# Reordering the work around three seams of a two-layer graph network: first batches, last attention batch with layer 1's first aggregate, and the last stages

## The chip, the cores and the metric

The kernel runs on one core of a Trainium2 chip. The metric is the device time of one execution in microseconds (us), lower is better. All arithmetic is float32. The engines are named as in the profile: PE is TensorE (matmul and transpose), PEld its weight loads, DVE is VectorE, ACT is ScalarE, POOL is GpSimd, and SP is the engine that issues most of the transfers (DMA). [...]

## The reference

The input x holds 16 batches of 1024 nodes with 256 channels; adj is one 1024 x 1024 matrix. Cut to what matters:

```
# layer 0
c_adj = mean of x over channels
A     = 2*| |sigmoid(c_adj[i]-c_adj[j]) - 0.5| - 0.5 |          # symmetrised
g     = relu((x^T @ (adj * A)) * para)                           # queries
k, v  = x @ kv_w
x     = layernorm(x + softmax(q @ k^T * scale) @ v)              # 4 heads of 64
# layer 1
A_norm = adj + I
dinv   = rsqrt(column sums + row sums - diagonal of A_norm)
A_hat  = A_norm * dinv[:, None] * dinv[None, :]
agg    = A_hat @ x
h      = relu(batchnorm(agg @ W1.T + b1))                        # 512 features
out    = batchnorm(h @ W2.T + b2)
return layernorm(x + out)
```

Both batchnorms take their statistics over all 16 x 1024 rows, so each of them is a point that all batches must have passed.

## The kernel before, in words

The tensors lie with 128 rows on partitions; a batch's x is a tile of 128 x 8 x 256 (1 MB). Score tiles are 128 x 1024 and take two PSUM banks; the others take one bank of 128 x 512. PSUM has three pools of two buffers each in the attention: s (scores and pg), t (transposes, keys, values, denominators) and o (attention outputs).

PE, ACT and DVE follow a written order (`manual_schedule`): their instructions run in the order in which the code emits them. SP and POOL follow theirs too, through the queues. So the order around the change is set by the loops of `run(list, k)`, which emit the next k steps of a list.

- **Start (L1144 to L1157).** `prologue(b)` (L757) makes three lists for a batch: `first` (`begin`, which sums x over channels on DVE at L772, writes the means to DRAM and reads them back as a row on all partitions at L779 and L781; and the four transposes of x, L788), `steps` (values L877, keys L864, then the graph matmuls L827) and `side` (the graph weights: ACT at L808 and L813, DVE at L817). Batch 0's and batch 1's lists are mixed here by hand; for batch 1 all of `side` is emitted before `steps`.
- **Attention.** A batch has two pairs of heads, two halves of queries and eight chunks of keys: 32 units, taken two at a time, so 16 bursts a batch (u = 0 to 15). A burst emits the scores of its two units (L924, exp on ACT at L929) and then the outputs of the burst before (L945, with the sums of the denominators on DVE, acc, L952 and L954). When all chunks of one half of the queries are done, outputs become oT (ACT copies one bank at L958, DVE adds the other at L959). `normalise` (L967) sums the denominators on PE, copies them on ACT and sends them through DRAM into columns (dcol). `residual` takes the reciprocal (L988), transposes oT (poT, L991), multiplies on DVE (o, L995) and adds to x on POOL (L1000). `statistics_x1` is the layernorm's bn_stats on DVE (16 small instructions, L614) and four POOL steps (L587 to L618, rs and nm); `finish_x1` applies it with 8 ACT instructions (L622) and stores the batch from POOL's queue (x1_d).
- **Last batch (b = 15).** The bursts carry, instead of a next batch, the preparation of layer 1, from the dict `last` (L1173): the transposes of the adjacency (`transpose_adjacency`, pah, L1071; ACT moves them to ahT at L1074 and sums the columns), the degrees (DVE L1081 to L1084, POOL's power at L589, and a row of dinv through DRAM), the transposes of W1 and W2 (pw, L1039 and L1048, copied to w12T by DVE), the identity's addition on POOL (L1093) and the scaling of ahT by dinv (`scale_adjacency`, DVE L1096, eight of them). The weights are loaded at u = 6 of b = 14.
- **First aggregate (L1252 to L1262).** `aggregate_first(m)` (pagg, L1123) sums batch 0 over the eight m, with scaling m+1 emitted before step m; the last denominators and residuals of b = 15 come at m = 1 and 4; `adjacency_sums` (aT, L691 to L694) and the layernorm of b = 15 come behind. ACT copies pagg to agg_0 (L1129).
- **Layer 1 loop (b = 1 to 15).** Strassen-like products of seven: `aggregate(b)` (a_agg, b_agg, c_agg, L1341) with the steps of `linear1(b - 1)` (a_h, b_h, c_h, L1373) mixed in, two a step; `linear1` begins with sums tT on DVE. h goes to DRAM by POOL's queue.
- **Second product.** The linear step of batch 15 (ph, L1452) is plain; `coefficients1` makes the batchnorm's scale and shift. Then, for each batch, h is loaded by SP (`load_h`, pool hl), scaled with relu on ACT (L1442), multiplied (po2 tiles, written po in the profile, L1512), moved by DVE with the bias (L1523), and summed for statistics (L1527).
- **Final stage.** For each batch: scale and shift on ACT (L1554), transposes back (pf, L1577) with x_1 added on DVE, or, for the other half, on PE (held, L1563 and L1592); layernorm coefficients in ten small POOL steps (L1604 to L1613); then two pieces of the result on DVE (L1620) and six on ACT (L1625), and one store of 1 MB from SP's queue (L1629).

## Time and profile before

| | |
|---|---|
| median of 3 runs | 2630.38 us (2630.32 to 2632.36) |
| profiled execution | 2630.78 us |
| its span | 2628.9 us |
| granted PE clock, mean | 0.996 |

The span splits into stages by the lines that run: the start up to about 76 us; batches to 1622; the last batch's bursts to 1703.6; the first aggregate to 1736.6; the layer 1 loop to 2286 (36.4 a batch); ph to 2301; the second product to 2526; the final stage to 2629.

How to read it. Times are microseconds from the span's start. In a row such as "L954 DVE TENSOR_TENSOR acc<-acc,p ... x384 | 484.7, 1262" the line number belongs to the listing above, the tile names are the program's, x384 is the count, 484.7 the busy time in total and 1262 the mean of one in nanoseconds. In a list of waits, "PE pah L1071 <- DVE o L995" says which instruction stood and whose end released it, followed by the total, the number of times and the longest. A busy PE is not PE at its peak, since matmuls overlap. Of the three engines that follow the written order, the page shows these groups with idle time before them:

```profile
L929 ACT ACTIVATE p<-ps 128x1024 f32<-128x1024 f32 x512 | 496.8, 1023 | 192.8 <-PE ps L924 161.7
L954 DVE TENSOR_TENSOR acc<-acc,p 128x1024 f32<-128x1024 f32 x384 | 484.7, 1262 | 126.9 <-ACT p L929 98.0
L924 PE MATMUL ps<-qT,kT 64*64 64x512 f32 x4096 | 490.6, 592 | 0.6 <-DVE qT L836 0.3
L945 PE MATMUL po<-p,v 64*64 64x512 f32 x4096 | 488.0, 589 | 0.0
```

### The profile page before, as it was taken

The page shows a single profiled execution, that of the slowest core. Times are in us where ns is not written, and L with a number is a line of the kernel's source. Part 1 is how long each engine was busy: PE and PEld are TensorE (multiplying, and loading weights), DVE is VectorE, ACT ScalarE, POOL GpSimd, SP SyncE. Part 2 cuts the span into 40 slices and gives each one's busy share as a digit, 9 for nine tenths or more (in the row PEclk, how much of TensorE's full clock was granted, in tenths as well). Part 3 has the DMA queues.
Part 4 walks back from the last instruction along what each step waited for, and adds up shares of the span by engine and source line. Part 5 has one row for each costly group of instructions (what it writes and reads, how often), then busy time and mean ns, then how long its engine had stood idle before and what let it go on. Part 6 is the DMA issues. An engine that isn't in the chain of part 4 may idle for free.

```text
span 2628.9 us, 32328 instructions
## 1 busy us (share of the span) xinstructions
PE 2565.4 (98%) x13158; PEld 1130.2 (43%) x13158; DVE 1515.3 (58%) x1941; ACT 1202.5 (46%) x1479; POOL 362.0 (14%) x439
## 2 busy tenths in 40 slices
PE   8999999999999999999999999999999999999986
PEld 4443443444434434444344444344444444444455
DVE  4365665655756646556566466766565565533367
ACT  6365564664655646646656564511010110133358
POOL 0010110101101101011011010331221122000035
PEclk9999999999999999999999999999999999999999
DMA  4001101011011011010110110111221222253458
GB/s 144 1 9 41 33 10 41 17 25 33 10 41 33 9 41 31 12 41 2 41 33 9 41 49 2 41 65 80 96 96 64 96 80 96 96 216 142 153 197 300
DMA packets 134559, 168.98 MB, mean 64 GB/s; under 512 B 86784, under 2 KB 120064, under 8 KB 124032
## 3 DMA queue, kind: packets, MB, share of 16 engines
q1 hardware_dynamic: 129568, 116.47, 14.0%
q0 software_dynamic: 4832, 50.34, 4.6%
q8 instruction: 105, 1.72, 0.3%
q14 instruction: 54, 0.44, 0.1%
HBM read 99.36 MB, written 67.44 MB: 63 GB/s over the span
## 4 chain that ended last, share of the span: by engine, by line
PE 83%; DVE 8%; ACT 6%; issue 1%; DMA 1%; POOL 0%; DVEq 0%; POOLq 0%; ACTq 0%
PE ps L924 16%; PE pg L827 16%; PE po L945 16%; PE po L1512 8%; PE pv L877 5%; PE b_agg L1341 4%; PE c_agg L1341 4%; PE pk L864 3%; PE b_h L1373 2%; PE a_agg L1341 2%; PE c_h L1373 2%; ACT o L1625 1%; ACT o L1554 1%; PE pxT L788 1%; PE den L967 1%
## 5 line engine op out<-in xcount | busy, mean ns | idle before, releaser
L929 ACT ACTIVATE p<-ps 128x1024 f32<-128x1024 f32 x512 | 496.8, 1023 | 192.8 <-PE ps L924 161.7
L954 DVE TENSOR_TENSOR acc<-acc,p 128x1024 f32<-128x1024 f32 x384 | 484.7, 1262 | 126.9 <-ACT p L929 98.0
L924 PE MATMUL ps<-qT,kT 64*64 64x512 f32 x4096 | 490.6, 592 | 0.6 <-DVE qT L836 0.3
L945 PE MATMUL po<-p,v 64*64 64x512 f32 x4096 | 488.0, 589 | 0.0
L827 PE MATMUL pg<-wg,x 128*128 128x512 f32 x960 | 420.9, 594 | 0.0
L1000 POOL TENSOR_TENSOR x<-x,o 128x512 f32<-128x512 f32 x64 | 123.1, 1924 | 1173.5 <-DVE o L995 1173.5
L945 PEld LDWEIGHTS po<-p,v 64*64 64x64 f32 x4096 | 159.9, 133 | 280.2 <-issue 271.5
L827 PEld LDWEIGHTS pg<-wg,x 128*128 128x128 f32 x960 | 178.9, 190 | 221.5 <-issue 208.5
L924 PEld LDWEIGHTS ps<-qT,kT 64*64 64x64 f32 x4096 | 152.6, 133 | 282.7 <-issue 254.4
L1512 PE MATMUL po<-hl,w12T 128*128 128x512 f32 x512 | 222.0, 596 | 3.4 <-DVE bn_st L1527 2.7
L836 DVE SCALAR_TENSOR_TENSOR qT<-pg,para_s 128x1024 f32<-128x1024 f32 (+1 forms) x34 | 39.2, 1160 | 236.2 <-PE pg L827 235.0
L817 DVE SCALAR_TENSOR_TENSOR wg<-wg,adj_s 128x1024 f32<-128x1024 f32 x128 | 162.1, 1278 | 22.9 <-ACT wg L813 22.9
L1512 PEld LDWEIGHTS po<-hl,w12T 128*128 128x128 f32 x512 | 97.7, 191 | 127.7 <-issue 120.9
L808 ACT ACTIVATE wg<-crow,ccol 128x1024 f32<-128x1024 f32 x128 | 147.1, 1150 | 9.3 <-DMA crow<-c 9.3
L813 ACT ACTIVATE wg<-wg 128x1024 f32<-128x1024 f32 x128 | 136.2, 1065 | 1.7
L1442 ACT ACTIVATE hl<-hl,bn_sh,bn_sg 128x1024 f32<-128x1024 f32 x64 | 74.3, 1229 | 137.1 <-DMA hl<-h 125.2
L877 PE MATMUL pv<-kvw_s,xT 128*128 128x256 f32 x512 | 126.9, 391 | 8.3 <-ACT kT L868 8.3
L959 DVE TENSOR_TENSOR oT<-po,oT 128x512 f32<-128x512 f32 x64 | 44.2, 691 | 145.6 <-ACT oT L958 145.6
L864 PE MATMUL pk<-xT,kvw_s 128*128 128x512 f32 x256 | 121.7, 598 | 3.3 <-ACT v L882 3.3
L1523 DVE TENSOR_SCALAR o<-po,col_b 128x1024 f32<-128x1024 f32 x31 | 39.8, 1284 | 137.9 <-PE po L1512 137.9
L622 ACT ACTIVATE x<-x,nm_l,rs_l 128x256 f32<-128x256 f32 x128 | 64.6, 587 | 111.4 <-POOL nm_l L618 111.4
L877 PEld LDWEIGHTS pv<-kvw_s,xT 128*128 128x128 f32 x512 | 92.6, 189 | 52.2 <-ACT kT L868 27.5
(163 smaller groups left out, 2698.0 us busy)
## 6 DMA issues: line engine op xcount, KB each, us to landing
h<-hw POOLq DMA_DIRECT2D x16, 2048.0 KB, 6.6
hl<-h SPq DMA_DIRECT2D x15, 2048.0 KB
x<-x POOLq DMA_DIRECT2D x16, 1024.0 KB, 4.2
x1l<-x SPq DMA_DIRECT2D x16, 1024.0 KB
xf<-x SPq DMA_DIRECT2D x16, 1024.0 KB
out_dram<-o SPq DMA_DIRECT2D x16, 1024.0 KB
x<-in_x_dram SPq DMA_DIRECT2D x15, 1024.0 KB
crow<-c SPq DMA_DIRECT2D x15, 512.0 KB
```

The costliest lines, as they stand in the source:

```text
L808: nc.scalar.activation(w, s["crow"], AF.Abs, bias=s["ccol"][:, n : n + 1])
L813: nc.scalar.activation(w, w, AF.Tanh, scale=0.5)
L817: nc.vector.scalar_tensor_tensor(w, w, 1.0, adj_s[:, n, :], op0=ALU.subtract, op1=ALU.mult)
L827: nc.tensor.matmul(s["pg"][:, hs], xt[:, n, c * P : (c + 1) * P], s["wg", n][:, hs], start=(n == 0), stop=(n == NCH - 1),)
L864: nc.tensor.matmul(ps, kvw_s[:, c, kc * P : (kc + 1) * P], s["xT"][:, c, hs], start=(c == 0), stop=(c == CC - 1),)
L877: nc.tensor.matmul(pt[:, j * C : (j + 1) * C], s["xT"][:, c, n * P : (n + 1) * P], kvw_s[:, c, C : 2 * C], start=(c == 0), stop=(c == CC - 1),
L924: nc.tensor.matmul(ps[kh * D : (kh + 1) * D, hd * HALF : (hd + 1) * HALF], kT[r, pr, ks], qT[r, pr, qh * HALF : (qh + 1) * HALF], start=Tr ...
L929: nc.scalar.activation(p, ps, AF.Exp)
L945: nc.tensor.matmul(g["po"][kh][hd * D : (hd + 1) * D, :], s["v"][r, m, h * D : (h + 1) * D], p[r, hd * HALF : (hd + 1) * HALF], start=(m = ...
L954: nc.vector.tensor_add(g["acc"], g["acc"], p)
L1341: nc.tensor.matmul(ps, left, right, start=(start and i == 0), stop=(i == NCH // 2 - 1), skip_group_check=True,)
L1512: nc.tensor.matmul(ps[:, hs], w2T[:, k, c * P : (c + 1) * P], h[k][:, hs], start=(k == 0), stop=(k == HC - 1),)
```

## The change

It moves instructions and splits a few of them; the sums that the kernel computes stay.

- Start: batch 1's `begin` is emitted after the fifth of batch 0's first eight steps; batch 1's steps and side work are emitted one and one.
- Last batch: one adjacency group (two halves) in each of the bursts 0 to 7; the weights' load at burst 1 of b = 15; residuals at bursts 2, 9 and 13; batch 14's statistics at burst 11 and its apply and store at burst 12; x1l loads at bursts 6 and 13; the scaling of m = 0 and 1 at burst 14, of m = 2 among the last outputs, of m = 3 to 7 at the first aggregate's first step. The aggregate's sums lie in single banks of the pools o and t, the last denominators and poT in pool s.
- Batch 15's statistics come right after the first aggregate; its apply, its store and the load of x1l_2 come in the first step of the loop's b = 1, and the linear steps of batch 0 start one step later (three of them in two of the steps).
- One `manual_schedule` spans all stages after the attention. ph is summed by halves; the pool hl is opened ahead of o2p; the first po2 batch takes k = 0, 1 of both channel groups, then k = 2, 3; the last channel group of the last batch is summed by halves.
- Final stage: the x_1 tiles 3 to 6 and 10 to 13 are loaded as pairs into hl's buffers. For batch 15, batch 14's `finish` comes ahead of its coefficients, which are made on DVE except for the power; DVE makes four pieces and ACT four; the store is split into two halves, from SP's and ACT's queue.

The diff, with what only moves by indentation or renames left out:

```diff
@@ outputs(i), L946
+            if i < len(units) - 1:
+                sums()
...
+            if i == len(units) - 1:
+                scale_adjacency(2)
+                sums()
@@ normalise, residual
+            den = tile_s("den_last")[:, H0] if last else tile_t(f"den_{k}")
...
+            if (b, pr) == (B - 1, PAIRS - 1):
+                pt = tile_s(f"poT_{k}")[:, H0]
@@ -1117,16 +1128,17 @@
                 agg[0] = xTp.tile([P, CC, N], F32, tag="xT", name="agg_0")
-                agg["ps"] = [tile_s(f"pagg_{c}") for c in range(CC)]
-            for c in range(CC):
-                for hs in (H0, H1):
+                agg["ps"] = [[tile(f"pagg_{i}") for i in range(2)] for tile in (tile_o, tile_t)]
+            for c in (1, 0):
+                for half, hs in enumerate((H0, H1)):
                     nc.tensor.matmul(
-                        agg["ps"][c][:, hs], x1l[0][:, m, c * P : (c + 1) * P], aht[m][:, hs],
+                        agg["ps"][c][half], x1l[0][:, m, c * P : (c + 1) * P], aht[m][:, hs],
...
             if m == NCH - 1:
-                for c in range(CC):
-                    nc.scalar.copy(agg[0][:, c, :], agg["ps"][c])
+                for c in (1, 0):
+                    for half, hs in enumerate((H0, H1)):
+                        nc.scalar.copy(agg[0][:, c, hs], agg["ps"][c][half])
@@ -1144,17 +1156,20 @@
             next_first, next_steps, next_side = prologue(1)
-            for _ in range(8):
+            for i in range(8):
...
                 run(side, 2)
-            run(next_first, 5)
+                if i == 4:
+                    run(next_first, 1)
+            run(next_first, 4)
...
                     run(next_side, 3)
-            run(next_side, 99)
-            run(next_steps, 8)
+            for _ in range(8):
+                run(next_steps, 1)
+                run(next_side, 1)
@@ -1170,20 +1185,14 @@
-            last = {
-                0: [(transpose_adjacency, (m, h)) for m in (0, 1) for h in (0, 1)],
-                4: [(transpose_adjacency, (m, h)) for m in (2, 3) for h in (0, 1)],
-                6: [(transpose_adjacency, (m, h)) for m in (4, 5) for h in (0, 1)],
-                8: [(transpose_adjacency, (m, h)) for m in (6, 7) for h in (0, 1)],
-                5: [(load_x1l, (0,))],
-                7: [(load_x1l, (1,))],
-                9: [(degrees, ())],
-                10: [(transpose_weights, ())],
-                12: [(add_identity, ())],
-                15: [(scale_adjacency, (0,))],
-            }
+            last = {u: [(transpose_adjacency, (u, h)) for h in (0, 1)] for u in range(NCH)}
+            for u, todo in (
+                (1, (load_weights,)), (6, (load_x1l, 0)), (9, (degrees,)), (10, (transpose_weights,)),
+                (12, (add_identity,)), (13, (load_x1l, 1)), (14, (scale_adjacency, 0)),
+                (14, (scale_adjacency, 1)),
+            ):
+                last.setdefault(u, []).append((todo[0], todo[1:]))
             before_last = {
-                6: [(load_weights, ())],
@@ -1206,14 +1215,14 @@
                         run(sums, 1)
-                    elif u in (2, 4, 12):
+                    elif u in (2, 9, 13):
                         run(full, 2)
-                    elif u == 5:
-                        run(late, 1)
-                    elif u == 7:
-                        run(late, 1)
...
                         run(sums, 1)
+                    elif u == 11:
+                        run(late, 1)
+                    elif u == 12:
+                        run(late, 1)
@@ -1250,16 +1259,22 @@
             for m in range(NCH):
-                if m + 1 < NCH:
-                    scale_adjacency(m + 1)
+                if m == 0:
+                    for k in range(3, NCH):
+                        scale_adjacency(k)
+                elif m < 4:
+                    adjacency_sums(m - 1)
+                elif m == 4:
+                    adjacency_sums(3)
...
                     run(full, 2)
-            for i in range(NCH // 2):
-                adjacency_sums(i)
-            run(late, 2)
+            late.clear()
+            x_last = st.pop(B - 1)["x"]
+            last_statistics, last_apply = layernorm_steps(x_last, f"l0_{B - 1}")
+            last_statistics()
@@ -1285,15 +1300,19 @@
+    manual = ExitStack()
+    manual.enter_context(tc.manual_schedule(engines={PE, Activation, DVE}))
@@ -1413,10 +1432,10 @@
         for b in range(1, B):
-            if b + 1 < B:
+            if 1 < b < B - 1:
...
                 x1_sums(b + 1)
-            else:
+            elif b == B - 1:
@@ -1427,7 +1446,13 @@
                     later = linear1(b)
-                run_linear(lin, 2)
+                if b > 1 or i > 0:
+                    run_linear(lin, 3 if b == 1 and i in (3, 5) else 2)
+                if b == 1 and i == 0:
+                    last_apply()
+                    nc.gpsimd.dma_start(x1_d[B - 1], x_last)
+                    load_x1l(2)
+                    x1_sums(2)
@@ -1447,21 +1472,21 @@
             ps = [bank(f"ph_{k}_{half}") for half in range(2)]
-            for c in range(CC):
-                for half, hs in enumerate((H0, H1)):
+            for half, hs in enumerate((H0, H1)):
+                for c in range(CC):
...
                     )
-            if k == HC - 1:
-                scale_shift1(h0[0], 0)
...
             coefficients1(k)
-        for k in range(1, HC):
+            if k > 1:
+                scale_shift1(h0[k - 2], k - 2)
+        for k in range(2, HC):
@@ -1472,7 +1497,7 @@
-    with tc.tile_pool(name="o2p", bufs=1) as o2p:
+    with tc.tile_pool(name="hl", bufs=2) as hl, tc.tile_pool(name="o2p", bufs=1) as o2p:
@@ -1484,51 +1509,61 @@
+            pss = [tile_s(f"po2_{b}_{c}") for c in range(CC)]
...
+            if b == 0:
+                for ks in (range(HC // 2), range(HC // 2, HC)):
+                    for c in range(CC):
+                        for k in ks:
+                            for hs in (H0, H1):
+                                mm(c, k, hs)
...
+                if b:
+                    for k, hs in (
+                        [(k, hs) for hs in (H0, H1) for k in range(HC)] if last
+                        else [(k, hs) for k in range(HC) for hs in (H0, H1)]
+                    ):
+                        mm(c, k, hs)
@@ -1537,15 +1572,20 @@
         with (
-            tc.tile_pool(name="fin2", bufs=4) as fin2,
...
             tc.tile_pool(name="ps_sum", bufs=2, space=PSUM) as ps_sum,
-            tc.manual_schedule(
-                engines={mybir.EngineType.PE, mybir.EngineType.Activation, mybir.EngineType.DVE}
-            ),
         ):
-            for b in range(3, 7):
-                load_x1(b, fin2, "xf")
+            pairs = {}
+
+            def load_x1_pair(b):
+
+                pairs[b] = hl.tile([P, 2, NCH, C], F32, tag="hl", name=f"xf_{b}_{b + 1}")
+                for i in range(2):
+                    xf[b + i] = pairs[b][:, i]
+                    nc.sync.dma_start(xf[b + i], x1_d[b + i])
+
+            load_x1_pair(3)
+            load_x1_pair(5)
@@ -1596,11 +1636,13 @@
                     nc.vector.bn_stats(st[:, n, :], held[b][:, (n - 4) * C : (n - 3) * C])
+                if b == B - 1:
+                    between()
...
                 rstd, nmr, dif, var = (w[:, k, :] for k in range(4))
-                pool = nc.gpsimd
+                pool = nc.vector if b == B - 1 else nc.gpsimd
@@ -1608,7 +1650,7 @@
                 pool.tensor_tensor(var, var, dif, ALU.add)
-                pool.tensor_tensor(rstd, var, mhalf, ALU.pow)
+                nc.gpsimd.tensor_tensor(rstd, var, mhalf, ALU.pow)
@@ -1616,33 +1658,44 @@
                 y = o2T[b].rearrange("p c n -> p (c n)").rearrange("p (n c) -> p n c", c=C)
-                for n in (0, 1):
+                last = b == B - 1
+                for n in (0, 1, 2, 3) if last else (0, 1):
...
                     )
-                for n in (4, 5, 6, 7, 2, 3):
+                for n in (4, 5, 6, 7) if last else (4, 5, 6, 7, 2, 3):
...
                     )
-                nc.sync.dma_start(out[b].rearrange("(n p) c -> p n c", p=P), y)
-                if b + 7 < B:
-                    load_x1(b + 7, *((fin2, "xf") if 3 <= b < 7 else (xp, "x")))
+                dst = out[b].rearrange("(n p) c -> p n c", p=P)
+                if last:
+                    nc.sync.dma_start(dst[:, M0, :], y[:, M0, :])
+                    nc.scalar.dma_start(dst[:, M1, :], y[:, M1, :])
+                else:
+                    nc.sync.dma_start(dst, y)
+                if b in (4, 6):
+                    load_x1_pair(b + 6)
+                elif b + 7 < B and not 3 <= b < 7:
+                    load_x1(b + 7, xp, "x")
...
             for b in range(B):
-                coeffs[b] = residual2(b)
+                def before(b=b):
+                    if b:
+                        finish(b - 1, *coeffs.pop(b - 1))
+
+                coeffs[b] = residual2(b, before)
...
                     scale_shift(b + 1)
-                if b:
-                    finish(b - 1, *coeffs.pop(b - 1))
+                    before()
...
-
+    manual.close()
```

## The prediction

> **What bounds the kernel now.** I read the page's first part, then the table of stretches, then TensorE's (PE's) waits, then the timelines of each engine where those waits fall.

> ```profile
> span 2628.9 us, 32328 instructions
> PE 2565.4 (98%) x13158; PEld 1130.2 (43%) x13158; DVE 1515.3 (58%) x1941; ACT 1202.5 (46%) x1479; POOL 362.0 (14%) x439
> ```

> PE is busy 2565.4 of 2628.9 us. The change takes no matmul away, so all it can win is a part of 63.5 us. Where these lie (columns: stretch, length, then busy us of PE, PEld, DVE, ACT, POOL):

> ```profile
> 0.00:76.00 76.00, 67.25 (x204) 37.80 (x208) 34.16 (x37) 42.92 (x49) 5.58 (x15) 0.98 0.37 125
> ...
> 1622.00:1703.60 81.60, 76.23 (x651) 31.43 (x643) 53.72 (x86) 48.72 (x78) 21.36 (x20) 1.00 0.13 34
> 1703.60:1736.60 33.00, 30.35 (x84) 12.81 (x80) 24.18 (x24) 3.19 (x4) 17.59 (x10) 1.00 0.05 3
> ...
> 2286.00:2301.00 15.00, 14.22 (x34) 6.19 (x33) 11.44 (x17) 6.97 (x10) 4.65 (x16) 1.00 0.33 140
> ...
> 2526.00:2629.00 103.00, 75.48 (x448) 56.27 (x448) 78.53 (x195) 82.25 (x131) 59.17 (x165) 0.93 0.81 297
> ```

> The last stretch has 27.5 of them and is paced by ACT (5.15 us a batch); the change leaves its loop alone. The seams it edits are the other rows: start, last attention batch, first aggregate, step to layer 1's second product. PE's waits name what ends each (total, times, longest):

> ```profile
> PE pv L877 <- ACT kT L868: 8.3, 29, 1.6
> ...
> PE po L1512 <- DVE bn_st L1527: 2.7, 1, 2.7
> PE pxT L788 <- ACT xT L792: 1.9, 1, 1.9
> PE pah L1071 <- DVE o L995: 1.9, 1, 1.9
> PE b_h L1373 <- DVE tT L692: 1.8, 1, 1.8
> PE pagg L1123 <- DVE ahT L1096: 1.6, 2, 1.3
> ...
> PE pah L1071 <- ACT ahT L1074: 1.3, 3, 0.8
> PE pah L1071 <- ACT drow L973: 1.1, 1, 1.1
> PE a_agg L1341 <- ACT agg L1129: 1.1, 1, 1.1
> PE po L1512 <- ACT hw L1459: 0.8, 1, 0.8
> ```

> **The change part by part.** Sums are made against the profiled execution: 2630.78 us, span 2628.9, so 1.9 lie around the span; the median 2630.38 is 0.4 below it.

> *Start.* Batch 1's sums over channels (DVE 2.27 us at 26.81) stand in front of the copy that frees a bank: pxT waits 0.24 + 1.92. Moved four steps ahead they lie in DVE's idle places of 1.6 to 2.8 us. The row of means then also leaves earlier (c was issued at 29.40, crow arrived for ACT at 43.45). With the graph weights and keys interleaved one to one, pv no longer waits 1.63 for a kT copy queued behind weights, nor ps 0.28. Sum 4.1, less one short restart: **-3.6**. Bounds: if x_1 had not landed at 22 us, DVE would block, and the gain would go to 0; x_1's load is issued at 2.83, behind 2.5 MB, so I take the gain. Range -4.2 to 0.

> *Last batch, bursts 0 to 7.* 1622.15 to 1665.39 is 43.2 us. Eight bursts of 3.43 are 27.4. Before there are six transposed groups in pairs; after, one group (8 transposes, about 1.05 with the switch: 1637.79 to 1638.81 for the same number) in each burst, and one residual instead of two: 27.4 + denominators 2.35 + residual 1.05 + 8 x 1.05 = 39.2. The 1.9, 0.78 and 0.34 of pah waits go. What is late next: at burst 2 the first half waits for DVE's second o (held by POOL's add, 1.26), the next for ACT's evacuation, about 0.35 + 0.7. So 40.3, **-2.8**. The weights' load, moved to burst 1, puts two SP issues (0.5 each) there; nothing of SP's waits behind them.

> *Bursts 8 to the last output (1665.39 to 1703.64, 38.25 us).* Work alone: 27.4 + 1.7 (last outputs) + 1.0 denominators + 2 x 1.05 residuals + about 2.7 weights' transposes = 35.3 (two groups of pah have left, one pair of residuals has come). Before, 1.7 us of waits lay here. After, the residuals of burst 9, the statistics of batch 14 (4.3 on DVE) of burst 11 and their apply (8 ACT, 4.03) of burst 12 come in where before there were none, and in a stretch where little but the bursts covers them. I laid DVE's queue out by the rows, zero at burst 8's scores: recip, o, (wait for POOL's add 1.3), o, degrees until 12.5; two acc sums (2.55) until 15.0; so the pw copies (0.65 each) are late and pw waits 1.6; next two sums until 20.2, statistics until 24.5, two sums and oT until 27.5; output 504 needs that bank: 1.7. The apply needs POOL's four steps, then stands in front of exp of 506, and scores 508 wait for its bank: 4.2. With 0.4 of small ones 7.9, so 43.2: **+4.9**.

> POOL's steps are the unsure term. The profile has them both ways: beside DVE's acc sums rs took 1.12, the power 2.68, nm 1.11 (5.4 in all), with DVE quiet about 0.25, 1.67, 0.20 (2.4). [...] It goes against this move: burst 11's statistics are followed by acc sums and oT. By the contended row the sum is +4.9; by the quiet row the apply starts 2.5 us earlier, +2.4. I take the contended one, since DVE's queue is full there. Lower end -1.5 (stalls only 1.4), upper end +8.

> *First aggregate (1703.64 to 1736.61, 32.97 us).* Work is 8 x 3.44 + 1.0 + 1.05 = 29.6. Scaling 0 to 2 lies ahead of it, 3 to 7 at its first step (five took 10.12, so each is done before its m, which takes 3.44): the 1.6 of pagg goes. The adjacency's sums come in steps 1 to 4 instead of behind. a_agg still waits for a copy, now 512 wide (0.58 to 0.75). 29.6 + 0.75 = 30.35: -2.6. The linear steps start one step later, so b_h doesn't wait for tT (1.8): together **-4.4**. Statistics and apply of batch 15 lie behind it; SP's load of x1l_2 then waits for their store (4.2 to land, 4.7 to load) and POOL's sums for that load, 9 of the 36 us until they are used, with no h store due on POOL before. SP's load of x1l_1 moves to burst 13 and waits for x_14's store; the denominators' transfers behind it are due 10 us later. Both free. Range -4.4 to 0, should DVE come late (see the rivals).

> *Step to the second product (2286 to 2301).* By halves, and with ph on a bank the next stage does not share first, po's 0.8 becomes about 0.3: -0.5. The 2.7: hl_1's load was issued at 2308.12, since its buffer lay where others had not ended; ACT's scaling began at 2316.08 and po waited. With hl opened ahead of o2p only an older h store is in front, which lets it go near 2285. Batch 0 by k halves gives the last scaling another 3.5 us. -2.7, together **-3.2**. Range -3.5 to -0.5.

> *To the final stage.* The last channel group by halves lets the second coefficients start 0.63 earlier; two pairs of x_1 loads go from 2512 on instead of 2525, into DMA that was idle until about 2529. The later pairs (10/11, 12/13) are issued after batches 4 and 6, about five periods before use. **-0.6**, range -1.5 to +1.

> *End.* Before: DVE statistics end 2614.27, POOL's ten steps 2614.42 to 2618.52, ACT six pieces to 2621.46, one store of 1 MB, span end 2628.9. After: batch 14's two pieces (0.72) stand ahead on DVE, then seven small steps on DVE (about 0.17 each), the power on POOL (1.67), two on DVE: ready 0.2 us earlier. Four ACT pieces (1.93) instead of six (2.92): 1.0. Together 1.15. The store is now two halves, from SP and ACT. [...] The trace: bytes moved from 2622.25 to 2625.5 at about 345 GB/s, so the whole MB cannot be faster, but DVE's half is ready about 0.6 earlier and starts then. I add 0.75: **-1.9**, range -1.1 to -2.5.

> Sum: -3.6 - 2.8 + 4.9 - 4.4 - 3.2 - 0.6 - 1.9 = **-11.6**, so 2619.2 for the profiled execution, **2618.8** for a median.

> **The rivals.**

> *A: the waits go and none comes.* For it: DVE is busy only 53.7 of the 81.6 us of the last batch, and before its acc waited 7.6 us for p. Against: that is an average, and bursts 9 to 12 have their DVE work in one row. Bursts 8 to the end then -1.5, the start -4.2: -11.6 - 6.4 - 0.6 = -18.6: **2611.8**.

> *B: the seams are only half worth it.* x_1 late at the start (0 instead of -3.6) or the last batch at its upper end (+8 instead of +4.9), some 3.3 either way, and hl_1 still behind another store (-0.5): -11.6 + 3.3 + 2.7 = -5.6: **2624.8**; with all three 2628.2. The change then does not do what it says in one of its three blocks.

> *C: slower.* DVE ends the last attention batch about 10 us late. Its queue takes everything in order, so each wait for POOL's add or ACT's copy in bursts 9 to 13 is handed on, and the scaling of m = 3 to 7, at 2 us each, falls behind pagg. Decided when the sum of acc for the last pair begins over 5 us after its exp: up to there the first three steps of pagg (10.3 us) cover two sums, oT and a scaling (5.3). Then the last batch costs +10 instead of +4.9 and the first aggregate +8 instead of -4.4: -11.6 + 5.1 + 12.4 = +5.9: **2636.3**. For it: all that moved is on DVE. Against: five scalings of 10.12 us fit 5 x 3.44.

> **How the numbers follow.** The forecast, 2615 to 2622, has 0.45; A, 2608 to 2615, 0.29; B 0.22, most of it at 2622 to 2628; C 0.04. 0.2% is 5.3 us, about what a measurement of this kernel can tell from no change: 2625.1 to 2635.6. Of B 0.12 lie above 2625.1. Faster 0.84, no difference 0.12, slower 0.04. The range runs from 2610 to 2626 and leaves out the rest of A, a part of B and C.

> **What would show it.** Start: no pxT wait on xT, none of 1.6 on pv. Last batch: pah waits under 1.2 in all; new PE waits of pw on w12T (1.6), po on oT (1.7) and ps on p (4.2) in bursts 9 to 14. If these are absent, A. pagg and b_h waits on tT gone; if pagg waits for ahT over 3 us, C. hl_1 issued near 2285 (shifted by what was won ahead) and no po wait on bn_st. At the end a store in two rows and 2 us less from the last statistics to the span's end. I would be wrong most easily in the +4.9.

## The result, and the profile after

Changed kernel: **2621.22 us** median (2620.78 to 2622.70, 7 runs) against 2630.32 (2629.50 to 2632.36, 7 runs) on the same chip, 9.1 us less; ratio 0.9966, 95% interval 0.9955 to 0.9978. It is faster by more than 0.2%, inside the predicted range, and 2.4 us above the forecast of 2618.8.

The page's first lines, of the kernel after:

```profile
span 2619.1 us, 32333 instructions
PE 2563.1 (98%) x13158; PEld 1128.8 (43%) x13158; DVE 1516.7 (58%) x1952; ACT 1201.4 (46%) x1479; POOL 358.5 (14%) x430
```

The span fell by 9.8 us, but PE's idle time only from 63.5 to 56.0: 2.3 us of the gain are *busy* time of the same 13158 matmuls. That was in no step of the prediction. 1.7 of it is one stretch of half clock fewer while PE has work: by the clock records, three in the trace before (from 30.65, 2317.58 and 2532.62) and two after (from 1695.03 and 2524.47), each 3.41 us long.

Where it came from: the times at which the same instruction starts in both traces, as differences (us). They come from one trace of each kernel.

| stretch | before | after | change | predicted |
|---|---|---|---|---|
| start to the first scores | 75.86 | 71.06 | -4.80 | -3.6 |
| from there to the first pah (batches 0 to 14) | 1552.12 | 1552.13 | 0 | 0 |
| first pah to burst 8's scores | 37.41 | 36.11 | -1.30 | -2.8 |
| burst 8's scores to first pagg | 38.25 | 45.36 | +7.11 | +4.9 |
| first pagg to second batch of the loop | 71.14 | 66.82 | -4.32 | -4.4 |
| from there to the first po | 525.92 | 525.93 | 0 | -0.5 |
| first po to the first held | 225.99 | 221.36 | -4.63 | -2.7 and -0.6 |
| to the end of the last statistics | 87.58 | 87.68 | +0.1 | 0 |
| to the span's end | 14.63 | 12.65 | -1.98 | -1.9 |

The sum is -9.8. (Burst 8's scores and the first pagg start at 1665.39 and 1703.64 before, at 1659.30 and 1704.66 after.) The start varies: in the nine experiments that keep the changed start, the first scores come at 71.03 to 72.37, so its gain is 3.5 to 4.8, and the trace here is at the favourable end.

PE's waits after (total, times, longest) answer to the list of before:

```profile
PE pv L877 <- ACT kT L868: 6.7, 28, 0.2
...
PE ps L924 <- ACT p L929: 3.8, 2, 3.6
...
PE pw L1059 <- DVE w12T L1053: 2.7, 1, 2.7
PE b_h L1392 <- DVE u_h L640: 1.5, 1, 1.5
...
PE pxT L788 <- DVE xT L792: 1.0, 2, 0.8
PE po L945 <- DVE oT L963: 1.0, 1, 1.0
PE pah L1082 <- ACT ahT L1085: 0.8, 1, 0.8
PE po L1530 <- ACT hw L1482: 0.8, 1, 0.8
PE a_agg L1360 <- ACT agg L1141: 0.7, 1, 0.7
PE pah L1082 <- DVE o L1006: 0.3, 1, 0.3
```

Gone are po on bn_st (2.7), b_h on tT (1.8), pagg on ahT (1.6), most of pah and the long one of pv. New are the three that were forecast: pw on w12T, po on oT, ps on p (3.6 of the 3.8; the other 0.3, at the start, was there before), and two small ones of pxT on DVE's xT. The wait of po on hw stands as it was, 0.8.

How the largest new wait comes about is seen in three timelines (start, duration, engine, line, tile; in brackets the idle time and its releaser). POOL's four steps for batch 14:

```profile
1684.69 1.12 POOL L587 TENSOR_SCALAR rs_l<-mv_l 128x8 f32<-128x8 f32 x1 [9.24 <-DVE mv_l L615]
1685.89 2.67 POOL L589 TENSOR_TENSOR rs_l<-rs_l,mhalf 128x8 f32<-128x8 f32 x1
1688.64 0.20 POOL L617 TENSOR_TENSOR nm_l<-mv_l,rs_l 128x8 f32<-128x8 f32 x1
1688.93 0.25 POOL L618 TENSOR_SCALAR nm_l<-nm_l 128x8 f32<-128x8 f32 x1
```

ACT's apply behind them, and the exps behind the apply:

```profile
1689.22 4.04 ACT L622 ACTIVATE x<-x,nm_l,rs_l 128x256 f32<-128x256 f32 x8 [4.30 <-POOL nm_l L618]
1693.16 1.91 ACT L929 ACTIVATE p<-ps 128x1024 f32<-128x1024 f32 x2
```

PE, which waits for a free score bank, and is slow behind it:

```profile
1687.69 1.94 PE L945 MATMUL po<-p,v 64*64 64x512 f32 x14 [0.95 <-DVE oT L963]
1689.56 1.09 PE L1002 MATMUL poT<-ident,oT 128*128 128x128 f32 x8
1694.21 2.94 PE L924 MATMUL ps<-qT,kT 64*64 64x512 f32 x16 [3.56 <-ACT p L929]
1696.91 2.66 PE L945 MATMUL po<-p,v 64*64 64x512 f32 x16
1699.40 1.90 PE L924 MATMUL ps<-qT,kT 64*64 64x512 f32 x16
```

DVE's statistics end at 1684.6; POOL is done at 1689.2, and the power beside DVE's acc sums takes 2.67, not the 1.65 to 1.67 of the final stage; ACT applies until 1693.2, and only then comes the exp whose bank the scores at 1694.21 need. These 16 matmuls and the next 16 take 2.70 and 2.49 us from start to start, where 1.71 is usual. The table of stretches says why (length, busy of PE, PEld, DVE, ACT, POOL, granted clock, DMA share, GB/s):

```profile
1691.00:1694.00 3.00, 0.00 (x0) 0.00 (x0) 0.06 (x1) 3.00 (x6) 0.45 (x1) 1.00 0.00 0
1694.00:1696.00 2.00, 1.78 (x12) 0.56 (x16) 0.47 (x1) 1.52 (x3) 1.47 (x2) 0.76 0.63 258
1696.00:1698.00 2.00, 2.00 (x16) 0.77 (x12) 1.90 (x3) 1.31 (x2) 1.70 (x1) 0.50 0.67 270
1698.00:1700.00 2.00, 2.00 (x21) 0.65 (x19) 2.00 (x2) 0.29 (x1) 0.48 (x1) 0.89 0.47 70
```

Behind the wait the granted clock is halved for a while: 0.24 x 2 + 0.5 x 2 + 0.11 x 2 = 1.7 us lost. In the kernel before, the same follows the 2.67 us wait of the second product; it lost 0.1 x 2 + 0.5 x 2 + 0.25 x 2 = 1.7 there:

```profile
2316.00:2318.00 2.00, 0.63 (x1) 0.33 (x2) 1.32 (x3) 1.92 (x2) 0.00 (x0) 0.90 0.99 426
2318.00:2320.00 2.00, 2.00 (x4) 0.74 (x3) 0.00 (x0) 2.00 (x3) 0.00 (x0) 0.50 0.94 401
2320.00:2322.00 2.00, 2.00 (x5) 0.94 (x4) 0.00 (x0) 1.81 (x2) 0.00 (x0) 0.75 0.99 414
```

Wait and slow clock together, 2.67 + 1.7 = 4.4, make up most of the 4.63 that the second product gave instead of 2.7.

### The profile page after: what moved, and what is told of

The parts are those of the page before. It is cut to its first block, busy times and chain, and to the rows that moved or that the text cites. A ratio compares the mean times of both kernels' runs of the same rounds, so it can differ in the third digit from the quotient of the medians.

```text
span 2619.1 us, 32333 instructions
## 1 busy us (share of the span) xinstructions
PE 2563.1 (98%) x13158; PEld 1128.8 (43%) x13158; DVE 1516.7 (58%) x1952; ACT 1201.4 (46%) x1479; POOL 358.5 (14%) x430
## 5 line engine op out<-in xcount | busy, mean ns | idle before, releaser
L836 DVE SCALAR_TENSOR_TENSOR qT<-pg,para_s 128x1024 f32<-128x1024 f32 (+1 forms) x34 | 39.2, 1161 | 236.7 <-PE pg L827 235.0
L877 PE MATMUL pv<-kvw_s,xT 128*128 128x256 f32 x512 | 126.8, 390 | 6.7 <-ACT kT L868 6.7
L839 ACT ACTIVATE qT<-qT 128x1024 f32<-128x1024 f32 (+1 forms) x34 | 34.1, 1007 | 175.2 <-DVE qT L836 175.2
```

The costliest lines, as they stand in the source:

```text
L877: nc.tensor.matmul(pt[:, j * C : (j + 1) * C], s["xT"][:, c, n * P : (n + 1) * P], kvw_s[:, c, C : 2 * C], start=(c == 0), stop=(c == CC - 1),
```

## The experiments

Theory S: the gain is what the removed waits cost, with the slow clock behind a long wait as part of a wait's price; 7 us of it are given back in bursts 9 to 14, because batch 14's residuals, statistics and apply were moved where nothing covers them. Rival P: DVE's total work limits the last batch wherever the pieces lie. Rival W: the slow clock comes by itself and no wait's removal changes it. All kernels start from the changed one unless another is named. "Against before" is the difference of medians to the kernel before on the same chip; the changed kernel has -9.1 there.

| kernel | median | against before | ratio to before, 95% |
|---|---|---|---|
| e1_apply_late | 2618.12 | -13.2 | 0.9937 to 0.9964 |
| e2_old_places | 2614.68 | -16.6 | 0.9924 to 0.9951 |
| e3_combo | 2616.03 | -15.2 | 0.9928 to 0.9955 |
| e4_hl_under | 2627.19 | -4.1 | 0.9978 to 0.9991 |
| e5_start_back | 2624.00 | -6.6 | 0.9967 to 0.9984 |
| e6_one_store | 2621.80 | -8.8 | 0.9957 to 0.9980 |
| e7_no_halves | 2620.85 | -9.8 | 0.9952 to 0.9979 |
| e8_single_residuals | 2611.65 | -19.0 | 0.9915 to 0.9943 |
| e9_pairs_of_groups | 2613.40 | -16.9 | 0.9920 to 0.9947 |
| e10_old_tail | 2623.16 | -7.2 | 0.9960 to 0.9983 |

The changed kernel's own interval is 0.9955 to 0.9978. Those of e1, e5, e6, e7 and e10 overlap it and e4's touches it, so for these the reading rests on the traces' stretches and waits, with one trace of each kernel.

**e1_apply_late.** The apply leaves the exps' way.

```diff
                     elif u == 11:
                         run(late, 1)
-                    elif u == 12:
-                        run(late, 1)
...
             back(j - 1)
+            run(late, 1)
```

> The changed kernel, with one thing moved: batch 14's apply and store (8 ACT steps) go behind the last attention output instead of burst 12. Theory S (the apply stands in front of the exps, PE's 3.6 us wait of scores on p follows from it, and the slow TensorE clock right after that wait, about 1.8 us, belongs to it): both go, 5.3 us faster than the changed kernel, about 2616; the clock stays at 1.00 from burst 8 on. Rival theory P (DVE's queue is the limit; what ACT no longer delays, the late o and acc delay): under 2 us faster, a new wait on oT or acc. Theory W (the slow clock came by itself and not from the wait): 3.6 us faster.

The stretch from burst 8 to pagg fell from 45.36 to 40.02: 5.3, wait and slow clock together, as S has it. But the waits show a new one:

```profile
PE pagg L1134 <- DVE oT L963: 1.7, 1, 1.7
```

In the trace the stretch from pagg to the second product grew by 2.4, and by the medians the gain is 4.1 us instead of 5.3. S holds for the wait itself, and a part of P for what follows it: PE now arrives ahead of DVE's last oT.

**e2_old_places.** Residuals, statistics and apply at the bursts of before.

```diff
-                    elif u in (2, 9, 13):
+                    elif u in (2, 4, 12):
...
-                    elif u == 11:
-                        run(late, 1)
-                    elif u == 12:
+                    elif u in (5, 7):
                         run(late, 1)
```

> The changed kernel, with batch 14's residuals, statistics and apply in the bursts where the kernel before had them (residuals at 2, 4 and 12, statistics 5, apply 7); the transposes stay one group a burst. Theory S (the stretch from burst 8 on grew by 7.1 us because these three were moved into it): the stretch returns to about 36.5, bursts 0 to 7 grow by about 2 (one residual more and its wait), net 6 to 7 us faster, about 2615. Rival (the transposes spread over eight bursts need just this free room of DVE and ACT, so the old waits of pah, 4.3 us, and a wait of scores on p behind the apply come back): between 2 us faster and 2 us slower, 2619 to 2623.

7.5 us less than the changed kernel. Burst 8 to pagg: 34.78 instead of 45.36, and the waits of ps on p and po on oT are gone from it. In the last batch these are the longest left, and pw's:

```profile
PE pah L1082 <- DVE o L1006: 1.7, 2, 1.3
PE pah L1082 <- ACT ahT L1085: 1.6, 2, 0.8
...
PE pw L1059 <- DVE w12T L1053: 0.3, 1, 0.3
```

So the moves cost 10.6 there, of which about 1 is a pair of residuals' own work on PE, and DVE was not the limit as such: P falls. In bursts 0 to 7 the profiled run paid 5.0 (36.11 to 41.15), more than the 2 expected; 1.7 of them are the clock, as the next run shows.

**e3_combo.** Residuals at 2, 4 and 13, statistics at 6, apply behind the last output.

```diff
-                    elif u in (2, 9, 13):
+                    elif u in (2, 4, 13):
...
-                    elif u == 11:
-                        run(late, 1)
-                    elif u == 12:
+                    elif u == 6:
                         run(late, 1)
...
             back(j - 1)
+            run(late, 1)
```

> The changed kernel with residuals at bursts 2, 4 and 13, statistics of batch 14 at burst 6 and its apply behind the last output. Theory S: no long wait is left in the last batch: bursts 0 to 7 grow by 2, the rest falls by 10, so 8 us faster, about 2613. Rival P (DVE): the weights' transposes still wait 2.7 for DVE, so 5 us faster at most, about 2616.

6.1 less than the changed kernel, not 8. pw's wait fell from 2.7 to 0.3, against P, but pagg waits 1.7 for oT as in e1. This run and e2 have the same two waits of pah in burst 4, 1.32 and 0.78. In e2:

```profile
1646.00:1649.00 3.00, 1.48 (x12) 1.00 (x10) 1.60 (x4) 0.60 (x2) 0.83 (x1) 1.00 0.00 0
1649.00:1652.00 3.00, 2.42 (x12) 1.16 (x16) 2.49 (x5) 1.22 (x4) 2.19 (x2) 0.62 0.00 0
1652.00:1655.00 3.00, 3.00 (x28) 0.83 (x20) 2.80 (x13) 2.05 (x2) 0.83 (x2) 0.81 0.00 0
```

and in e3:

```profile
1646.00:1649.00 3.00, 0.90 (x6) 0.58 (x6) 1.60 (x5) 0.69 (x2) 1.27 (x1) 1.00 0.00 0
1649.00:1652.00 3.00, 3.00 (x28) 1.23 (x31) 1.91 (x3) 2.10 (x4) 2.50 (x2) 1.00 0.00 0
1652.00:1655.00 3.00, 3.00 (x32) 1.42 (x28) 2.86 (x5) 1.79 (x5) 0.10 (x1) 1.00 0.03 5
```

The clock falls to 0.62 in one and stays at 1.00 in the other, with equal waits. The last section shows where the two differ.

**e4_hl_under.** Only the order of two pools is put back.

```diff
-    with tc.tile_pool(name="hl", bufs=2) as hl, tc.tile_pool(name="o2p", bufs=1) as o2p:
+    with tc.tile_pool(name="o2p", bufs=1) as o2p, tc.tile_pool(name="hl", bufs=2) as hl:
```

> The changed kernel with the pool hl opened after o2p, as before. The second product's load of h_1 waits again. Theory S (a long wait of PE is followed by a slow clock, which is part of its price): 2.7 us of wait and 1.5 to 2 of slow clock, so 4.6 slower, about 2625.8. Rival W (the slow clock came by itself): 2.7 slower, about 2623.9. That the order of the pools does nothing: 2621.2.

5.0 slower than the changed kernel (-4.1 against -9.1). SP issues the load at 2306.91 instead of 2281.21. PE waits 4.30, not the expected 2.7: ACT's scaling begins at 2316.09, as it did before the change (2316.08), but PE has come 1.6 earlier:

```profile
2299.08 14.00 PE L1530 MATMUL po<-hl,w12T 128*128 128x512 f32 x32 [0.78 <-ACT hw L1482]
2317.39 13.12 PE L1530 MATMUL po<-hl,w12T 128*128 128x512 f32 x26 [4.30 <-ACT hl L1467]
```

```profile
2316.00:2319.00 3.00, 1.61 (x3) 0.84 (x4) 0.00 (x0) 2.91 (x3) 0.00 (x0) 0.84 0.95 410
2319.00:2322.00 3.00, 3.00 (x5) 1.19 (x4) 0.00 (x0) 2.81 (x3) 0.00 (x0) 0.59 1.00 415
```

The second product took 6.27 more in the trace, 4.30 of wait and 0.16 x 3 + 0.41 x 3 = 1.7 of clock, with a rest of 0.3; the final stage was 1.5 shorter in that profile and 1.4 in e9's: these two lack the 3.41 us of half clock that the other ten profiles have 4 to 6 us behind the first held. W as it stands is out: the wait goes and comes with this line, and the slow clock with it.

**e5_start_back.** Batch 1's `begin` back behind the first eight steps.

```diff
                 run(side, 2)
-                if i == 4:
-                    run(next_first, 1)
-            run(next_first, 4)
+            run(next_first, 5)
```

> The changed kernel with batch 1's begin put back behind batch 0's first eight steps (the interleaving one to one stays). Theory S (waits of about 2 us within a short stretch are followed by about 3 us of half clock): the waits of pxT, 2.2 us instead of 1.2, come back and with them the slow clock of about 1.4 us seen at 31 to 35 us before: 2 to 3 us slower, about 2623.7. Rival W (the slow clock at the start has nothing to do with it): 1 us slower, 2622.2. Rival: the later row of means delays the weights too, then pv or pk waits come back and it is 4 us slower.

2.5 slower than the changed kernel: the wait of pxT on xT is 1.9 again, pv's does not come back, and at 28 to 32 us the clock is 0.65:

```profile
28.00:32.00 4.00, 2.75 (x10) 2.23 (x11) 2.77 (x6) 1.94 (x4) 0.00 (x0) 0.65 0.12 1
32.00:36.00 4.00, 4.00 (x10) 1.73 (x9) 1.37 (x2) 1.92 (x2) 0.00 (x0) 0.92 0.02 4
```

The first scores come at 73.32, against 71.03 to 72.37 in the ten traces with the changed start. So 1.0 to 2.3 of the start's gain belong to this line. The rest is put down to the interleaving, which no run put back alone.

**e6_one_store.** The last store in one piece.

```diff
-                if last:
-                    nc.sync.dma_start(dst[:, M0, :], y[:, M0, :])
-                    nc.scalar.dma_start(dst[:, M1, :], y[:, M1, :])
-                else:
-                    nc.sync.dma_start(dst, y)
+                nc.sync.dma_start(dst, y)
```

> The changed kernel with the last batch's result stored by one transfer from SP instead of two halves from SP and ACT. By the prediction's step the split is worth 0.75 us: 2622.0. [...] From the last statistics to the span's end: 13.4 against 12.65.

0.3 slower by the medians, less than the intervals can tell, and 0.5 by the traces: 13.15 against 12.65, and the eight other traces with the split lie within 0.1 of the latter. The half that DVE makes is ready only 0.56 before ACT's (issues at 1.73 and 2.29 past 2610), so the data start to move about that much earlier: by the traces' slices they are over 300 GB/s from 2612.75 with the split and from 2613.24 without. The movement itself is at about 340 GB/s either way. The 0.75 was my estimate and a little too much.

**e7_no_halves.** Three orders of matmuls put back.

```diff
-            for half, hs in enumerate((H0, H1)):
-                for c in range(CC):
+            for c in range(CC):
+                for half, hs in enumerate((H0, H1)):
...
-                for ks in (range(HC // 2), range(HC // 2, HC)):
+                for ks in (range(HC),):
...
-                        [(k, hs) for hs in (H0, H1) for k in range(HC)] if last
+                        [(k, hs) for k in range(HC) for hs in (H0, H1)] if last
```

> The changed kernel with the sums of ph and of the last po2 group in the old order (not by halves), and the first po2 batch with all k of a channel group in one go. My step gave the halves 0.5 and 0.6; the trace after shows po's wait on hw (0.78) and held's on o (1.36) unchanged, so theory S: no difference from the halves, 2621.2. The k order of the first batch: if the last scaling of h_0 lands too late without it, po waits 0.3 to 1.5 for hl: up to 2622.7.

No difference; po's wait on hw (0.78) and held's on o (1.36) are the same in both. In the changed kernel ACT takes the two halves of the last po2 tile at once, after PE's last matmul has ended (2517.41), though the first half's sum was complete four matmuls of 0.43, some 1.7 us, before. Why it waits for both halves no run shows:

```profile
2517.45 1.27 ACT L1553 ACTIVATE o<-po,col_b 128x512 f32<-128x512 f32 x2 [14.42 <-PE po L1530]
```

**e8_single_residuals.** One residual a burst, two scalings earlier, batch 14's statistics at burst 7 and its apply behind the last output.

```diff
-                (12, (add_identity,)), (13, (load_x1l, 1)), (14, (scale_adjacency, 0)),
-                (14, (scale_adjacency, 1)),
+                (12, (add_identity,)), (13, (load_x1l, 1)), (12, (scale_adjacency, 0)),
+                (13, (scale_adjacency, 1)),
...
-                    elif u in (2, 9, 13):
-                        run(full, 2)
+                    elif u in (2, 3, 4, 5, 12, 13):
+                        run(full, 1)
...
-                    elif u == 11:
-                        run(late, 1)
-                    elif u == 12:
+                    elif u == 7:
                         run(late, 1)
...
             back(j - 1)
+            run(late, 1)
```

> The changed kernel with one residual a burst (2, 3, 4, 5 for batch 14; 12, 13 for batch 15), statistics of batch 14 at burst 7, its apply behind the last output, scaling of m = 0 at burst 12 and m = 1 at burst 13. Theory S (second o of a pair waits for POOL's add and pah for that o; DVE's last oT is late for pagg because the two scalings stand in front): the waits of pah fall from 3.3 to under 1 and that of pagg on oT from 1.7 to 0, so 3 to 4 us less than with pairs of residuals, about 2612. Rival: DVE's work only moves, and the wait turns up again as scores on p or po on oT: 2615 to 2616.

S's number came, about 2612: 3.8 less than e3. Of its two terms one held, pagg no longer waits for oT. The other did so in part: pah's waits fell from 3.3 to 2.0, not under 1. The rival's waits, of scores on p or po on oT, did not come. All that PE waits for in the last batch and the first aggregate:

```profile
PE pah L1082 <- DVE o L1006: 1.2, 3, 0.4
PE pah L1082 <- ACT ahT L1085: 0.8, 1, 0.8
PE a_agg L1359 <- ACT agg L1141: 0.7, 1, 0.7
PE pw L1059 <- DVE w12T L1053: 0.3, 1, 0.3
PE den L975 <- DVE acc L955: 0.3, 1, 0.3
```

It is the fastest kernel here by the medians, 19.0 less than the kernel before and 9.9 less than the changed one; its interval overlaps those of e2 and e9. What each of the moves in it brings is not separated.

**e9_pairs_of_groups.** The kernel e8 with the transposes in pairs of groups, as before the change.

```diff
-            last = {u: [(transpose_adjacency, (u, h)) for h in (0, 1)] for u in range(NCH)}
+            last = {
+                u: [(transpose_adjacency, (m, h)) for m in (2 * g, 2 * g + 1) for h in (0, 1)]
+                for g, u in enumerate((0, 4, 6, 8))
+            }
```

> The kernel with single residuals (label e8), with the adjacency's transposes back in pairs of groups at bursts 0, 4, 6 and 8. Theory G (one group a burst is worth something by itself, since two t banks and ACT's evacuation, 0.8 each, take four halves in a row only with waits): the waits of pah of about 0.8 at bursts 4, 6 and 8 and that for drow at 8 come back, minus four switches saved (about 0.15 each), 1.5 to 2.5 slower than e8, about 2613.7. Rival N (the spread is worth nothing once the residuals are apart): 2611.7. If the slow clock falls behind these waits in some runs, up to 1.7 more in those.

2.1 slower than e8 by the differences to before, near G's number. But the intervals overlap, and from the first pah to pagg the traces show only 74.15 against 73.38. The waits that G named came back in part: three of pah on ahT, 1.3 in all instead of about 2.4, none for drow, and e8's three for o (1.2) are gone. So one group a burst seems worth 0.8 to 2 us by itself, and neither that nor what pays it is shown. The cost of bursts 8 to 14 came from what was moved, not from the transposes (e2).

**e10_old_tail.** The end as before.

```diff
-                if b == B - 1:
-                    between()
...
-                pool = nc.vector if b == B - 1 else nc.gpsimd
+                pool = nc.gpsimd
...
-                for n in (0, 1, 2, 3) if last else (0, 1):
+                for n in (0, 1):
...
-                for n in (4, 5, 6, 7) if last else (4, 5, 6, 7, 2, 3):
+                for n in (4, 5, 6, 7, 2, 3):
```

with one store as in e6.

> The changed kernel with the end as before: the last coefficients on POOL, two pieces of the last batch on DVE and six on ACT, batch 14's finish behind the coefficients, one store. The prediction's step: 1.9 slower, 2623.1, of which 1.15 are from the shorter way to the last piece and 0.75 from the split. By the run with one store (split worth 0.5) the rest is 1.4. From the last statistics to the span's end 14.6 against 12.65. Rival: the coefficients on DVE bring nothing (2614.42 to 2618.52 on POOL before), only two ACT pieces fewer: 1.0 + 0.5 = 1.5 slower.

1.9 slower by the medians (-7.2 against -9.1), 1.6 by the traces (14.27 against 12.65), so the total does not tell the step's 1.9 from the rival's 1.5. The trace does: behind the last statistics the last batch's pieces begin after 3.9 us with the coefficients on DVE and after 4.3 on POOL. DVE brings 0.4, not nothing, and two ACT pieces fewer bring 1.0. The end was rightly sized; the split is the smaller part of it.

## Why the prediction was right, step by step

The sign, the range and the three new waits held, but that the sum came so close is in part luck. By the traces the sum was 1.8 us too large: +1.5 and +2.2 in the last batch and +1.1 for halves that gave nothing, against -1.2 and -1.9 where the clock was won as well. No step had a term for the clock, which gave 1.7 at the start and 1.7 in the second product and took 1.7 in the last batch. Without the two misses in its favour the median would have been about 2624, above the forecast's 2622 though still inside the range. Two of the sums are also off in themselves: the terms of bursts 0 to 7 give -3.0, not -2.8, and the work of bursts 8 on adds to 34.9, not 35.3, which makes +4.5 of +4.9.

- *Start*, -3.6: measured -4.8. The pv wait (1.6) went; the pxT waits fell only from 2.2 to 1.2, with a new 0.78 on DVE's xT, and the 0.3 of ps stayed. So waits alone gave 2.6. What made up for it is the clock: 0.78 and 0.66 at 29 to 35 us before, 1.00 after, which is 1.7; the last 0.5 lie within the start's scatter. The lower bound, x_1 not landed, did not come.
- *Bursts 0 to 7*, -2.8: measured -1.3. The waits were right (0.35 and 0.78). The term that was mis-sized is the insertion: a group of eight in a burst of its own lengthens it by 1.19 (1640.83 to 1645.45 is 4.62, less 3.43), not 1.05; eight of them make 1.1 of the 1.5.
- *Bursts 8 to the last output*, +4.9: measured +7.1. The three waits came in their places: pw 2.7 (said 1.6), po on oT 0.95 (1.7), ps 3.56 (4.2), in all 7.2 for 7.5. Mis-sized was the price of the last: the slow clock behind it, 1.7. Of POOL's two rows in the trace before, the long one, beside DVE's acc sums, was the right one to take for rs and the power (1.12 and 2.67); nm took the short 0.20. What makes a step longer beside the acc sums is not shown.
- *First aggregate*, -4.4: measured -4.3.
- *Step to the second product*, -3.2: the load's order gave -4.6 with the clock; the halves' 0.5 gave nothing.
- *To the final stage*, -0.6: nothing. The step took for granted that ACT starts on a finished half; it started at 2517.45, behind both (e7).
- *End*, -1.9: measured -2.0.

Of the rivals, A was possible all the same, but not by this change: e8, which puts the same pieces elsewhere, is at A's time (2611.65 against 2611.8). C did not come near: pagg never waited for ahT.

## What to carry to other kernels

When a queue's work is moved, lay out every engine's queue from there on by the trace's durations: averages (DVE 53.7 of 81.6 us busy) said there was room, but in bursts 9 to 13 the moved work made PE wait 7.2 us, and back in bursts 0 to 7 it cost less (e2). What stands in front of a step that another engine waits for in every round (here an apply of 4.04 us in front of exps) belongs behind the last round. And two residuals with one buffer are not two steps: the second o waits for POOL's add of the first (1.3). Nor were two halves of one tile: ACT began on the first at 2517.45, when both were done (e7).

## What I had not expected of the hardware

I laid PE's matmuls into these windows, from its first to its last, transposes counted as work. 23 windows have 2.10 us or more without work, and a half clock follows each of them (2.11, 2.67 and 2.10 in the trace before, 2.60 and 2.20 in the one after); the other 9102 have 1.86 or less, and none follows. So equal waits cost differently in these traces. pw's wait of 2.70 in the changed kernel lies across an edge, 1.35 us on each side, and the clock stays at 1.00; in e4's profile 2.2 us of the same wait lie in one window. Two windows of the changed kernel:

```profile
1671.14:1674.55 3.41, 2.06 (x20) 1.01 (x12) 3.24 (x5) 0.51 (x1) 2.90 (x2) 1.00 0.00 0
1674.55:1677.96 3.41, 2.06 (x16) 1.20 (x20) 3.26 (x6) 0.00 (x0) 0.90 (x1) 1.00 0.14 1
```

and two of e4:

```profile
1672.93:1676.34 3.41, 1.19 (x12) 0.86 (x8) 3.24 (x6) 0.00 (x0) 2.90 (x2) 1.00 0.00 0
1676.34:1679.75 3.41, 2.93 (x16) 2.00 (x20) 2.63 (x5) 0.00 (x0) 0.02 (x1) 0.50 0.14 1
```

The half clock followed pw's wait in two of the seven profiles that have it, and ps's wait of 3.56 in all six. The 1.32 + 0.78 us put 2.10 into one window in e2 and at most 1.55 in e3. The medians' runs have no traces of their own, so whether the clock makes their scatter (2629.50 to 2632.36 before) is not shown.
